# Closing stretch of a fused attention block: two more softmax-sum turns on TensorE, and a last chunk multiplied without token mixing

## The chip, the cores and the metric

The kernel runs on one core of one Trainium2 chip. The metric is the device time of that core in microseconds. Three runs of the kernel before gave 1424.36, 1424.47 and 1426.91 us, so the median is 1424.47 us.

## What is computed

The reference is a transformer block with adaptive layer normalisation, over 8 batches of 1024 tokens with 256 features, all in fp32. Cut to what matters here:

```python
h = _layernorm(x) * (1 + ca) + sa
x = x + ga * attention(h)              # 16 heads of 16, causal, w_out, b_out
h = _layernorm(x) * (1 + cb) + sb
x_prev = h shifted by one token (zero before the first)
xr = mu_r * h + (1.0 - mu_r) * x_prev
xk = mu_k * h + (1.0 - mu_k) * x_prev
r = sigmoid(xr @ W_r)
k_act = square(relu(xk @ W_k))
x = x + gb * (r * (k_act @ W_v))
```

`sa, ca, ga, sb, cb, gb` come from a small modulation matmul per batch. The softmax divides by the sum of the exponentials of a row; the kernel carries that sum as a seventeenth row beside the 16 rows of each head's output.

## The kernel before, in words

Tokens of a batch are cut into two chunks of 512 (`c` = 0, 1), heads into four groups of four (`g`); one group of one batch is a unit `u`, 32 in all. The unit's work is cut into steps. A maxima step (`maxima`) multiplies queries by keys into `pp` and lets VectorE (DVE) take the row maxima; a weights step (`weights`), nine steps later, multiplies again into `pw`, and ScalarE (ACT) makes exponentials `w` of it. `attend` multiplies `w` by the values into `po`; its sums go into a tile `o`. TensorE (PE) takes its instructions strictly in program order.

The program is a list of slots. In each slot `step` issues one weights step and one maxima step of a later unit, then what fell due in `soon`, then the slot's filling from hand-written tables (`PREP`, `POST`, `END`: the number is a slot, the name a piece of work), then `attend` of the step before. DMAs wrapped in `later` are issued at the start of the next slot. The last two units are `y` = 30 and `z` = 31, groups 2 and 3 of the last batch; their steps are interleaved and cut by `GROUPS_APART`. Slot 289 is the last with a maxima step; slots 290 to 298 hold weights steps alone.

The division by the softmax sum is made in one of two ways. `gather` writes `o` to DRAM and reads it back in another layout into `oT`; `spread_sums`, `invert`, `write_over`, `read_over` carry the sums through DRAM, and `divide` multiplies `oT` on GpSimd (POOL). `gather_last` stays on the chip: TensorE transposes `o` into `psum`, VectorE inverts the sums (`inv`) and widens them (`wide`), TensorE turns them back (`pinv`), VectorE multiplies `o`, and four DMAs put its heads into `oT`. Before the change only chunk 1 of units `y` and `z` goes the second way.

`post` then is the second half of the block for one chunk: `project` (`py`), statistics, normalisation (`hb`), `turn` (transposes `ptb`, then `h2T`), `mix` (the difference of neighbouring tokens, `step`, on POOL), `mixed` (the two mixtures on DVE: receptance in `mix`, key written over `step`), `receptance` (`pr`), `key` (`pk`, then the square on POOL) and `value` (`pkv`). Chunk 0 of the last batch is placed by `END` at slot 261 + n, its keys and values after the last slot. Chunk 1 has its own function `tail`, run last of all and worked in halves of 256 tokens so that engines overlap: `py`, statistics, `pt_last`, `h2T_last`, mixing on DVE, `pr`, `pk_last`, `pkv_last`, output.

PSUM has four one-bank buffers (`ps_t`) that `pw`, `po`, `py`, `pr`, `pk`, `pkv`, `psum` and `pinv` take in rotation, and two double ones (`ps_s`) for `pp`. A matmul whose bank has not been read out yet waits, and all matmuls behind it wait with it.

Of the kernel before, what the change touches and what calls it, by code (L numbers as in the profile page):

```python
# [69 lines left out]
def adaln_block(  # L70
# [24 lines left out]
    def bank(name):  # L95
        return ps_t.tile([P, CW], F32, tag="t", name=name)
# [38 lines left out]
    def later(f, steps=1, urgent=False):  # L135

        if strict[0]:
            due.append((clock[0] + steps, not urgent, f))
        else:
            f()  # L140
# [542 lines left out]
    def gather_last(u, c):  # L683

        o = U[u]["o", c]
        b, g = divmod(u, NG)
        pt = bank(f"psum{u}")
        for t in range(NT):
            pe.transpose(pt[:, t * P : (t + 1) * P], o[:, t * P : (t + 1) * P], ident)
        inv = sb.tile([P, NT, HG], F32, tag="few", bufs=2, name=f"inv{u}")  # L690
        dve.reciprocal(inv, pt.rearrange("p (t j s) -> p t j s", t=NT, s=ST)[:, :, :, HD])
        wide = sb.tile([P, NT, HG, ST], F32, tag="over", bufs=2, name=f"wide{u}")
        dve.tensor_copy(wide, inv.unsqueeze(3).to_broadcast([P, NT, HG, ST]))
        po = bank(f"pinv{u}")
        for t in range(NT):
            pe.matmul(
                po[:, t * P : (t + 1) * P],
                wide[:, t].rearrange("p j s -> p (j s)"),
                ident,
                start=True,  # L700
                stop=True,
            )
        dve.tensor_mul(o, o, po)
        for j in range(HG):
            at = (g % 2) * HG * HD + j * HD
            queue = act if j % 2 and u == B * NG - 1 else sync
            queue.dma_start(
                A[b, c]["oT"][at : at + HD, g // 2, :], o[j * ST : j * ST + HD, :]
            )

    def spread_sums(b, c, d):

# [24 lines left out]
    def divide(b, c, d):  # L737
        S = A[b, c]
        pool.tensor_mul(S["oT"][:, d, :], S["oT"][:, d, :], S["over", d])


    def post(b, c):
# [90 lines left out]
        def tail():  # L833

            def both(f):
                f(0)
                f(1)

            def columns(half):
                return slice(half * CW // 2, (half + 1) * CW // 2)

            both(lambda half: project(2 * half))
            st = sb.tile([P, NT, 6], F32, tag="st", bufs=2, name="st_last")
            mv = sb.tile([P, NT, 2], F32, tag="mv", bufs=2, name="mv_last")
            rs = sb.tile([P, NT], F32, tag="rs", bufs=2, name="rs_last")
            h = sb.tile([P, NT, D], F32, tag="h", bufs=2, name="h_last")

            def normal(half):  # L850
                ts = (2 * half, 2 * half + 1)
                for t in ts:
                    dve.bn_stats(st[:, t, :], S["x"][:, t, :])
                    dve.bn_aggr(mv[:, t, :], st[:, t, :])
                of = slice(2 * half, 2 * half + 2)
                dve.tensor_scalar_add(rs[:, of], mv[:, of, 1], EPS)
                pool.tensor_tensor(rs[:, of], rs[:, of], m_half[:, of], ALU.pow)
                for t in ts:
                    dve.tensor_scalar(
                        h[:, t, :],  # L860
                        S["x"][:, t, :],
                        mv[:, t, 0:1],
                        rs[:, t : t + 1],
                        ALU.subtract,
                        ALU.mult,
                    )

            both(normal)
            h2T = sb.tile([P, DC, CW + 1], F32, tag="h2T", name="h2T_last")
            pool.tensor_copy(h2T[:, :, 0:1], A[b, 0]["edge"])  # L870

            def turned(half):
                pt = bank(f"pt_last{half}")
                for d in range(DC):
                    for n in range(2):
                        pe.transpose(
                            pt[:, (d * 2 + n) * P : (d * 2 + n + 1) * P],
                            h[:, 2 * half + n, d * P : (d + 1) * P],
                            ident,
                        )  # L880
                for d in range(DC):
                    act.activation(
                        h2T[:, d, 1 + half * CW // 2 : 1 + (half + 1) * CW // 2],
                        pt[:, d * CW // 2 : (d + 1) * CW // 2],
                        AF.Identity,
                        bias=modT[:, SHIFT_B, d, b : b + 1],
                        scale=modT[:, SCALE_B, d, b : b + 1],
                    )

            both(turned)  # L890
            step = sb.tile([P, DC, CW], F32, tag="step", name="step_last")
            S["mix"] = sb.tile([P, DC, CW], F32, tag="mix", bufs=2, name="mix_last")

            def mixed_half(half):
                of = columns(half)
                for d in range(DC):
                    dve.tensor_sub(
                        step[:, d, of],
                        h2T[:, d, 1 + half * CW // 2 : 1 + (half + 1) * CW // 2],
                        h2T[:, d, of],  # L900
                    )
                for n in range(2):
                    for d in range(DC):
                        dve.scalar_tensor_tensor(
                            (S["mix"], step)[n][:, d, of],
                            step[:, d, of],
                            mus[:, n, d : d + 1],
                            h2T[:, d, of],
                            ALU.mult,
                            ALU.add,  # L910
                        )

            both(mixed_half)
            S["ka"] = sb.tile([P, DC, CW], F32, tag="mix", bufs=2, name="ka_last")

            def keys(half):
                of = columns(half)
                pk = bank(f"pk_last{half}").rearrange("p (e n) -> p e n", e=DC)
                for e in range(DC):
                    for d in range(DC):  # L920
                        pe.matmul(
                            pk[:, e, :],
                            wk_sb[:, d, e * P : (e + 1) * P],
                            step[:, d, of],
                            start=(d == 0),
                            stop=(d == DC - 1),
                        )
                ka = S["ka"][:, :, of]
                act.activation(ka, pk, AF.Relu)
                dve.tensor_mul(ka, ka, ka)  # L930

            both(lambda half: (receptance(2 * half), keys(half)))

            def values(half):
                t0 = 2 * half
                pv = bank(f"pkv_last{half}")
                rows(pv, S["ka"], G[b]["wv"], (t0, t0 + 1))
                r = S["r", t0]
                dve.scalar_tensor_tensor(r, r, 1.0, pv, ALU.add, ALU.mult)
                dve.tensor_add(flat(t0), flat(t0), r)  # L940
                (sync, act)[half].dma_start(
                    tokens(out, b, c)[:, t0 : t0 + 2, :], S["x"][:, t0 : t0 + 2, :]
                )

            both(values)

        return dict(
            load=load_xb,
# [60 lines left out]
    def finish(T, now):  # L1009
        u, k = T  # L1010
        attend(u, k)
        c, _, ends = groups_of(u)[k]
        if ends:
            b, g = divmod(u, NG)
            if u >= B * NG - 2 and c:
                soon.append((now + 1, lambda: gather_last(u, c)))
                return
            soon.append((now + 1, lambda: gather(u, c)))
            if g % 2:
                for n, f in enumerate((spread_sums, invert, write_over, read_over)):  # L1020
                    soon.append((now + 2 + n, lambda f=f: f(b, c, g // 2)))
                soon.append((now + 7, lambda: divide(b, c, g // 2)))
# [48 lines left out]
    22 m.k1; 22 n.q1; 24 n.k1; 26 n.v0; 28 n.v2  # L1071
    """
    END = """
    26 x.load; 28 x.bias; 32 x.project0; 32 x.project2; 33 x.stats0; 33 x.stats1; 34 x.norm0;
    34 x.norm1; 35 x.turn; 35 x.mix; 36 x.mixed00; 36 x.mixed01; 36 x.mixed10; 36 x.mixed11;
    36 y.load; 37 y.bias; 37 x.receptance0; 37 x.receptance2
    """

    def place(table, at, **of):
# [32 lines left out]
    for b in range(B):  # L1112
# [10 lines left out]
            fold0=lambda b=b: fold(b, 0),  # L1123
            fold1=lambda b=b: fold(b, 1),
        )
    place(END, at, x=ready[b][0], y=ready[b][1])


    mask = const.tile([P, CW], F32, tag="mask", name="mask")
# [60 lines left out]
        while soon and soon[0][0] <= clock[0]:  # L1190
            soon.pop(0)[1]()
    strict[0] = False
    for f in ("key0", "key1", "value0", "value2"):
        ready[B - 1][0][f]()
    ready[B - 1][1]["tail"]()

# [51 lines left out]
```

## Time and profile before

| what | value |
|---|---|
| median of three runs | 1424.47 us |
| the profiled execution's own time | 1423.17 us |
| its span, first to last instruction | 1421.4 us |
| PE busy in the span | 1392.2 us (98%) |
| DVE, ACT, POOL busy | 1059.2, 896.5, 548.7 us |
| mean granted TensorE clock | 0.992 |

The profile was taken in one execution. "Busy" counts the time in which an engine had an instruction in work; matmuls are pipelined, so a matmul's row is longer than the time from its start to the next start. An fp32 matmul leaves two records. PEclk is the share of full TensorE clock that was granted in a stretch. Line numbers in the trace are all L112, the line of the helper that records every instruction; so the rows are told apart by tile names. The rows of the timeline give start, duration, engine, operation, output and inputs, number of instructions, and in brackets the engine's idle time before them and what released it.

### The profile page before, as it was taken

The numbers are of one execution on the slowest core, as the hardware profiler recorded it, in microseconds if no ns is written. First come the engines' busy times: TensorE is split into PE (matmuls) and PEld (weight loads), VectorE is DVE, ScalarE is ACT, GpSimd is POOL, SyncE is SP. The second block draws the span as 40 slices with busy tenths as digits, with TensorE's granted clock in tenths as the row PEclk, the third lists the DMA queues.
The fourth block names the chain that finished last, engine by engine and source line by source line (L and its number), as shares of the span: only waits on it lengthen the run. The fifth ranks groups of instructions, "written<-read, shape, count | busy, mean of one in ns | idle before, by whom it ended". The sixth has DMA issues, their size and how long they took to land.

```text
span 1421.4 us, 29731 instructions
## 1 busy us (share of the span) xinstructions
PE 1392.2 (98%) x11256; PEld 736.5 (52%) x11256; DVE 1059.2 (75%) x2869; ACT 896.5 (63%) x1693; POOL 548.7 (39%) x840
## 2 busy tenths in 40 slices
PE   8999999999999999999999999999999999999997
PEld 4544455555554555555554555545555555455455
DVE  6777687788777877787777887777787877787334
ACT  3466676666676666666666666666667665576541
POOL 1142242445423454434424354234543343345441
PEclk9999999999999999999999999999999999999998
DMA  6513323222222323222242222223232221301111
GB/s 191 177 36 89 123 76 113 62 101 80 94 69 75 107 83 99 73 91 73 76 128 62 95 83 89 75 76 107 69 102 63 76 93 61 99 32 36 47 34 33
DMA packets 81270, 118.95 MB, mean 84 GB/s; under 512 B 10208, under 2 KB 38752, under 8 KB 81128
## 3 DMA queue, kind: packets, MB, share of 16 engines
q1 hardware_dynamic: 80792, 116.74, 25.9%
q8 instruction: 88, 1.44, 0.4%
q14 instruction: 54, 0.44, 0.1%
q10 hardware_dynamic: 336, 0.33, 0.1%
HBM read 71.17 MB, written 45.09 MB: 82 GB/s over the span
## 4 chain that ended last, share of the span: by engine, by line
PE 93%; DVE 3%; POOL 1%; ACT 1%; issue 1%; DMA 0%; ACTq 0%; POOLq 0%; SPq 0%; DVEq 0%
PE pw L112 11%; PE po L112 8%; PE pq L112 8%; PE pp L112 7%; PE po_e L112 5%; PE po_c L112 5%; PE py L112 4%; PE pkv L112 4%; PE pr L112 4%; PE pv L112 4%; PE pk L112 4%; PE pw_a L112 3%; PE pw_c L112 3%; PE pw_d L112 3%; PE pw_e L112 2%; PE pmx L112 2%
## 5 line engine op out<-in xcount | busy, mean ns | idle before, releaser
L112 DVE TENSOR_REDUCE max<-pp 128x2 f32<-128x1024 f32 x256 | 302.3, 1219 | 127.3 <-PE pp L112 126.3
L112 ACT ACTIVATE w<-pw 128x512 f32<-128x512 f32 x512 | 265.1, 603 | 88.9 <-PE pp L112 71.0
L112 PE MATMUL pw<-q,k 32*128 32x512 f32 x1024 | 265.5, 616 | 0.4 <-ACT w_i L112 0.4
L112 PE MATMUL pp<-k,q 32*128 32x512 f32 x1024 | 255.7, 620 | 0.0
L112 PEld LDWEIGHTS pw<-q,k 32*128 32x128 f32 x1024 | 110.4, 183 | 104.7 <-issue 64.2
L112 DVE CUSTOM_DVE_ANT_0 pp_d<-pp_d,mask 128x128 f32<-128x128 f32 x240 | 102.4, 437 | 64.4 <-PE pp_d L112 58.2
L112 DVE DVE_READ_ACCUMULATOR2_ANT max<- 128x1 f32 x1024 | 144.8, 141 | 0.0
L112 PE MATMUL po<-w,v 128*32 128x512 f32 x1024 | 123.1, 598 | 0.0
L112 DVE CUSTOM_DVE_ANT_0 pp_b<-pp_b,mask 128x128 f32<-128x128 f32 x240 | 102.4, 437 | 16.8 <-PE pp_b L112 10.1
L112 PE MATMUL pq<-hT,wqk_sb 128*128 128x512 f32 x240 | 113.7, 606 | 1.0 <-ACT hT L112 1.0
L112 DVE CUSTOM_DVE_ANT_0 pp_c<-pp_c,mask 128x256 f32<-128x256 f32 x240 | 103.2, 440 | 8.3 <-PE pp_c L112 2.2
L112 DVE CUSTOM_DVE_ANT_0 pp_e<-pp_e,mask 128x512 f32<-128x512 f32 x128 | 87.9, 708 | 20.4 <-PE pp_e L112 18.1
L112 DVE CUSTOM_DVE_ANT_0 pp_a<-pp_a,mask 128x512 f32<-128x512 f32 x128 | 87.9, 707 | 16.9 <-PE pp_a L112 14.7
L112 POOL TENSOR_TENSOR xb<-xb,r 128x512 f32<-128x512 f32 x30 | 41.4, 1378 | 141.0 <-DVE r L112 115.9
L112 ACT ACTIVATE w_a<-pw_a 128x512 f32<-128x512 f32 x128 | 66.2, 603 | 41.6 <-PE pp_a L112 40.3
L112 POOL TENSOR_TENSOR o<-o,more 128x512 f32<-128x512 f32 x62 | 79.1, 1276 | 26.1 <-ACT more L112 26.1
L112 POOL TENSOR_TENSOR rsb<-rsb,m_half 128x2 f32<-128x2 f32 x30 | 21.4, 714 | 169.0 <-DVE rsb L112 168.9
L112 PEld LDWEIGHTS pp<-k,q 32*128 32x128 f32 x1024 | 82.7, 183 | 6.1 <-DVE max L112 5.6
L112 ACT ACTIVATE w_e<-pw_e 128x512 f32<-128x512 f32 x128 | 66.3, 604 | 14.1 <-PE pp_e L112 13.3
L112 ACT ACTIVATE w_c<-pw_c 128x512 f32<-128x512 f32 x120 | 64.8, 596 | 16.3 <-PE pp_c L112 14.5
L112 ACT ACTIVATE w_d<-pw_d 128x512 f32<-128x512 f32 x120 | 62.3, 602 | 16.6 <-PE pp_d L112 12.9
L112 ACT ACTIVATE w_b<-pw_b 128x512 f32<-128x512 f32 x120 | 62.0, 603 | 16.8 <-PE pp_b L112 16.3
(207 smaller groups left out, 3031.9 us busy)
## 6 DMA issues: line engine op xcount, KB each, us to landing
od<-o SPq DMA_DIRECT2D x62, 256.0 KB
pad<-qk SPq DMA_DIRECT2D x60, 256.0 KB
q<-pad SPq DMA_DIRECT2D x30, 512.0 KB
k<-pad SPq DMA_DIRECT2D x30, 512.0 KB
xa<-in_x SPq DMA_DIRECT2D x16, 512.0 KB
xb<-in_x SPq DMA_DIRECT2D x16, 512.0 KB
oT<-od SPq DMA_DIRECT2D x62, 128.0 KB
ov<-over SPq DMA_DIRECT2D x31, 256.0 KB
```

Of the source, the lines that this page charges most:

```text
L112: made = f(*args, **kwargs)
```

## The change

`gather_last` now serves chunk 0 of units `y` and `z` too; for chunk 0 its four DMAs are issued one slot later. So the sums of that pair no longer go through DRAM, and `divide` falls away for it. The `END` table is moved forward: chunk 0 projects in slots 288 and 289 instead of 293, and its keys come in slots 297 and 298 instead of after the last slot; the load and the bias of its `x` come six slots earlier as well.

In `tail` the mixing is dropped. `folded`, in slot 294, makes four weight tiles on DVE: W_r and W_k times mu, and times one minus mu. Key and receptance are then sums of two products each, one with the tokens and one with the tokens before. The order on TensorE becomes: six filler matmuls (`warm`), transposes and keys of half 0, transposes and keys of half 1, then receptance and values of each half.

```diff
@@ gather_last
-        for j in range(HG):
-            at = (g % 2) * HG * HD + j * HD
-            queue = act if j % 2 and u == B * NG - 1 else sync
-            queue.dma_start(
-                A[b, c]["oT"][at : at + HD, g // 2, :], o[j * ST : j * ST + HD, :]
-            )
+        def side_by_side():
+            for j in range(HG):
+                at = (g % 2) * HG * HD + j * HD
+                queue = act if j % 2 and c and u == B * NG - 1 else sync
+                queue.dma_start(
+                    A[b, c]["oT"][at : at + HD, g // 2, :], o[j * ST : j * ST + HD, :]
+                )
+        if c:
+            side_by_side()
+        else:
+            later(side_by_side)
@@ new, before post
+    by_mu = []
+    def folded():
+        rest = sb.tile([P, 2, DC], F32, tag="rest", name="rest")
+        dve.tensor_scalar(rest, mus, -1.0, 1.0, ALU.mult, ALU.add)
+        for n, of in enumerate((wr_sb, wk_sb)):
+            both = sb.tile([P, DC, CW], F32, tag="hT", bufs=2, name=f"by_mu{n}")
+            pair = []
+            for m, factor in enumerate((mus, rest)):
+                w = both[:, :, m * D : (m + 1) * D]
+                for d in range(DC):
+                    dve.tensor_scalar_mul(w[:, d, :], of[:, d, :], factor[:, n, d : d + 1])
+                pair.append(w)
+            by_mu.append(pair)
@@ tail
-            both(turned)
-            step = ...; S["mix"] = ...
-            def mixed_half(half): ...          # 2 differences, 4 mixtures on DVE
-            both(mixed_half)
+            def here_and_before(half, d):
+                at = half * CW // 2
+                return h2T[:, d, 1 + at : 1 + at + CW // 2], h2T[:, d, at : at + CW // 2]
             def keys(half):
...
-                        pe.matmul(
-                            pk[:, e, :],
-                            wk_sb[:, d, e * P : (e + 1) * P],
-                            step[:, d, of],
-                            start=(d == 0),
-                            stop=(d == DC - 1),
-                        )
+                        for m, tokens_of in enumerate(here_and_before(half, d)):
+                            pe.matmul(
+                                pk[:, e, :],
+                                by_mu[1][m][:, d, e * P : (e + 1) * P],
+                                tokens_of,
+                                start=(d == 0 and m == 0),
+                                stop=(d == DC - 1 and m == 1),
+                            )
-            both(lambda half: (receptance(2 * half), keys(half)))
+            def receptances(half):             # 2 x DC x 2 matmuls of 128x256, then tanh
...
+            warm(6, "warm1")
+            turned(0)
+            keys(0)
+            turned(1)
+            keys(1)
-            both(values)
+            both(lambda half: (receptances(half), values(half)))
@@ finish
-            if u >= B * NG - 2 and c:
+            if u >= B * NG - 2:
                 soon.append((now + 1, lambda: gather_last(u, c)))
                 return
@@ END
-    26 x.load; 28 x.bias; 32 x.project0; 32 x.project2; 33 x.stats0; 33 x.stats1; 34 x.norm0;
-    34 x.norm1; 35 x.turn; 35 x.mix; 36 x.mixed00; 36 x.mixed01; 36 x.mixed10; 36 x.mixed11;
-    36 y.load; 37 y.bias; 37 x.receptance0; 37 x.receptance2
+    20 x.load; 22 x.bias; 27 x.project0; 28 x.project2; 29 x.stats0; 29 x.stats1; 30 x.norm0;
+    30 x.norm1; 30 y.load; 31 x.turn; 31 x.mix; 32 x.mixed00; 32 x.mixed01; 32 y.bias; 33 x.mixed10;
+    33 x.mixed11; 33 w.folded; 34 x.receptance0; 35 x.receptance2; 36 x.key0; 37 x.key1
@@ after the slots
-    for f in ("key0", "key1", "value0", "value2"):
+    for f in ("value0", "value2"):
```

In the `END` table `x` is chunk 0 and `y` chunk 1 of the last batch; these letters are not the units y and z.

More of the change, by code (lines that the diff above doesn't have):

```diff
@@ L888, in turned @@
                     )
-            both(turned)
[L891 to L897, printed above, removed]
-                        step[:, d, of],
-                        h2T[:, d, 1 + half * CW // 2 : 1 + (half + 1) * CW // 2],
-                        h2T[:, d, of],
-                    )
[L902 to L911, printed above, removed]
-            both(mixed_half)
+            def here_and_before(half, d):
+                at = half * CW // 2
+                return h2T[:, d, 1 + at : 1 + at + CW // 2], h2T[:, d, at : at + CW // 2]
             S["ka"] = sb.tile([P, DC, CW], F32, tag="mix", bufs=2, name="ka_last")
             def keys(half):
-                of = columns(half)
                 pk = bank(f"pk_last{half}").rearrange("p (e n) -> p e n", e=DC)
@@ L920, in keys @@
                     for d in range(DC):
-                        pe.matmul(
-                            pk[:, e, :],
-                            wk_sb[:, d, e * P : (e + 1) * P],
-                            step[:, d, of],
-                            start=(d == 0),
-                            stop=(d == DC - 1),
-                        )
-                ka = S["ka"][:, :, of]
+                        for m, tokens_of in enumerate(here_and_before(half, d)):
[6 more added lines that the diff above has]
+                            )
+                ka = S["ka"][:, :, columns(half)]
                 act.activation(ka, pk, AF.Relu)
                 dve.tensor_mul(ka, ka, ka)
-            both(lambda half: (receptance(2 * half), keys(half)))
+            def receptances(half):
+                pr = bank(f"pr_last{half}")
+                for n in range(2):
+                    for d in range(DC):
+                        for m, tokens_of in enumerate(here_and_before(half, d)):
+                            pe.matmul(
+                                pr[:, n * D : (n + 1) * D],
+                                tokens_of[:, n * P : (n + 1) * P],
+                                by_mu[0][m][:, d, :],
+                                start=(d == 0 and m == 0),
+                                stop=(d == DC - 1 and m == 1),
+                            )
+                r = sb.tile([P, CW], F32, tag="r", bufs=2, name=f"r_last{half}")
+                act.activation(r, pr, AF.Tanh, scale=0.5)
+                S["r", 2 * half] = r
+            warm(6, "warm1")
[3 more added lines that the diff above has]
+            keys(1)
             def values(half):
@@ L1125, in adaln_block @@
         )
-    place(END, at, x=ready[b][0], y=ready[b][1])
+    place(END, at, x=ready[b][0], y=ready[b][1], w=dict(folded=lambda: folded()))
     mask = const.tile([P, CW], F32, tag="mask", name="mask")
```

## The prediction

> **What bounds the kernel now.** I read the page's busy shares first, then the timeline of PE and DVE over the last 120 us, then the clock in stretches of 2 us, then the chain that ended last.
>
> ```profile
> PE 1392.2 (98%) x11256; PEld 736.5 (52%) x11256; DVE 1059.2 (75%) x2869; ACT 896.5 (63%) x1693; POOL 548.7 (39%) x840
> ```
>
> PE is the bound: work moved from one place of its queue to another saves nothing, work added costs its length, and only PE's idle time and slow clock can be won. Two stretches of the timeline show where VectorE runs behind PE:
>
> ```profile
> 1300.37 0.60 PE L112 MATMUL pmx<-ident,max 128*4 128x128 f32 x4
> 1301.96 0.70 DVE L112 CUSTOM_DVE_ANT_0 pp_e<-pp_e,mask 128x512 f32<-128x512 f32 x1
> 1302.58 0.14 DVE L112 DVE_READ_ACCUMULATOR2_ANT max<- 128x1 f32 x1
> ...
> 1314.17 2.36 DVE L112 TENSOR_REDUCE max<-pp 128x2 f32<-128x1024 f32 x2 [0.75 <-PE pp L112]
> 1314.30 0.59 PE L112 MATMUL pp<-k,q 32*128 32x512 f32 x2
> ```
>
> Slot 283's maxima products leave PE at 1300.44 (where the chain of waits lets pmx begin) and DVE at 1302.72; slot 286's leave PE at 1314.89 and DVE at 1316.5. What `gather_last` costs is seen where unit z runs it today:
>
> ```profile
> 1383.61 0.66 PE L112 MATMUL psum<-ident,o 128*128 128x128 f32 x4 [0.87 <-DVE o L112]
> 1384.31 0.26 DVE L112 RECIPROCAL inv<-psum 128x16 f32<-128x16 f32 x1 [0.75 <-PE psum L112]
> 1384.60 0.43 DVE L112 COPY wide<-inv 128x512 f32<-128x512 f32 x1
> 1385.17 1.13 PE L112 MATMUL pinv<-ident,wide 128*128 128x128 f32 x8 [0.90 <-DVE wide L112]
> ```
>
> PE stands 0.90 us between psum and pinv although DVE was free. The clock in 2 us stretches (columns: PE, PEld, DVE, ACT, POOL busy, then PEclk):
>
> ```profile
> 1340.00:1342.00 2.00, 2.00 (x3) 0.79 (x3) 0.00 (x0) 0.84 (x2) 0.66 (x1) 0.54 0.00 0
> 1366.00:1368.00 2.00, 2.00 (x6) 1.64 (x5) 0.00 (x0) 0.82 (x2) 0.75 (x2) 0.50 0.00 0
> 1404.00:1406.00 2.00, 2.00 (x6) 1.55 (x6) 2.00 (x6) 0.81 (x2) 0.00 (x0) 0.50 0.00 0
> ```
>
> Three times near the end PE works at half clock. The end of the chain:
>
> ```profile
> 1403.75 3.67 PE pr L112 x8
> 1407.42 2.28 PE pk_last L112 x8
> 1409.70 1.73 PE pr L112 x8
> 1411.43 1.73 PE pk_last L112 x8
> 1413.16 3.47 PE pkv_last L112 x16
> ```
>
> Eight records (four 128x256 matmuls) take 1.73 us at full clock, so 0.433 us a matmul; the first pr and pk pay 2.5 us for half clock.
>
> **The change, marker by marker.** I follow PE's queue and note its shift, after minus before.
>
> *First new turn, slot 283.* The changed order puts psum and pinv behind the slot's pp_e, and `inv` behind pp_e's reductions on DVE. Four transposes take 0.53 (as the four pmx), PE is done at 1300.97; `inv` starts when DVE is free, 1302.72; plus 0.29 to wide, 0.43, 0.14 to PE: pinv starts at 1303.58. PE stands 2.6 us. Pinv to the next matmul is 0.97: 1304.55. Shift **+4.1**. DVE's multiply of o waits for pinv, with mix and the next maxima queued behind it, so nothing is won back: pmx, pk, the buffer `step` that POOL may write only after pk, mix on DVE and the wait of pp_i for it (0.93 today) all move along. POOL gets the bias of x there (2.79, today in slot 289) ahead of w_g's masks; they end at about 1315.3 against PE's need at 1316.3: hidden with 1 us to spare, and costing what exceeds that. SP's four extra DMAs (0.58 each) stand behind the urgent mrow and before the `ov` read of the other chunk, which is needed microseconds later: nothing (2.3 if they stood in the way). The load of x, moved past the `over` write on SP, is issued near 1292, 20 us before its bias: nothing.
>
> *Second, slot 286.* PE is done with psum at 1319.0 + 0.53, DVE with the reductions at 1316.5 + 4.1 = 1320.6; plus 0.86 is 1321.46 and plus 0.97 is 1322.43, against 1314.89: **+7.5**, 1.9 us of it standing.
>
> *Slots 288, 289.* Both halves of py come here, 1.73 each; the oT DMAs (issued until about 1325.6) land before PE's 1330.9. The first py gives DVE time: pw_e and pp_3 took 2.80 instead of a usual 1.93, I take 0.87 back. **+10.1** at po_3.
>
> *Slots 290 to 293.* Normalisation now stands on ACT between w_i and the next exponentials, and pk (slot 292) needs the bank that the first of those frees. On POOL the square of ka (done 1337.40, so 1347.5) is followed by the two pow chains; today they take 1360.13 to 1362.71, so 1350.1. Two hb (0.98) end at 1351.2, the first exponential at 1351.8. Pk starts at 1351.85 instead of 1339.88: 1.84 us of new standing, **+12.0**. At full clock pk takes 1.73 instead of 3.42 (-1.7); ptb moves in (+1.0): **+11.3** at po_i. POOL's `step` (2.03) now stands before `o`, psum waits 0.7 longer: **+12.0**. Without py (-3.46), **+8.5** at pw in slot 294. DVE's eight weight products (3.0 us, at h_last's 0.74 for two) and the mixtures lie under slots 293 to 295, where DVE is mostly idle, and are ready some 25 us before the tail: nothing, 3.0 without that cover.
>
> *Slots 295, 296.* Today 1359.72 to 1370.90 (11.2): two pw steps bound by ACT with hb among them, 1.30 standing, pkv at half clock (3.78), ptb. With pr between the steps, ACT keeps up: 1.85 + 1.73 + 1.85 + 1.93 + 1.73 = 9.1. **+6.4**. *Slots 297, 298:* two pk (3.46) for two pr (3.65) and a wait of 0.54: **+5.8** when po_i ends (1382.74).
>
> *To the tail.* The turn to pinv's end takes 3.58 as today, then pk (3.46) and the waits for POOL's ka (1.2) are gone. But py now catches up with its DMAs: o was done at 1387.03 and the last packets moved in 1389.50 to 1389.75, 7.0 after po_i; pkv ends at 7.04. I allow 0.3 standing; py ends 10.9 after po_i instead of 15.6: **+1.1**.
>
> *The tail.* Today py's end (1398.35) to pkv_last's end (1416.45) is 18.1. After: first transposes 1.64 after py as today (the six warm matmuls, 1.3, fit in), ACT 0.9 later, 0.5 for the first half of h2T: keys start at 3.05. Then PE: keys 3.46, transposes 0.45, h2T 0.65, keys 3.46, receptance 3.46, values 1.73, receptance 3.46, values 1.73: 21.45. The mixing and the half clock are gone, but eight keys and eight receptance matmuls (6.9 us) are new: **+4.4**. The last add and the DMA are the same.
>
> So +4.4 with no half clock after 1300, against three such stretches today.
>
> **A rule against the trace.** The clock row first: at 1340 it fell to 0.54 though PE had stood only 0.44 us in the stretch before (ahead of pw, 1337.2 to 1337.6); what ran before were pw steps of 32 rows without pp. The Trainium skill, "TensorE: Matmul & The Clock Gate", section "HAM oscillation", says to avoid PE-idle gaps above about 3.4 us. By that rule the new stands of 2.6, 1.9 and 1.84 us cost no clock: +4.4. By the row, the low stretch of pw_i and pw_0 followed by 1.84 us of standing drops the clock as today, and pk gets its 1.7 back: **+6.1**. I follow the trace. A gap of 2.6 or 1.9 us among joint steps has no row (the 0.93 at 1305.7 left the clock at 1.00): each costs between 0 and 1.7, one half-clock stretch of 3.4 us like 1340 to 1343.3; a gain is excluded, since standing cannot raise a full clock. I take 0 for these, as the nearest row (0.93) says, and keep 3.4 for the range. Standing of 1.7 before the keys, with transposes in it, lies between 1.24 (0.28 and 0.96 before 1349.5, clock 1.00) and the 5.3 from 1398.35 to 1403.67, transposes inside, that dropped it today; I take full clock there, too, with 3.4 as the bad end.
>
> The profiled execution took 1423.17 with a span of 1421.4; the median is 1.3 above it. On the median: 1424.5 + 6.1 = **1430.6**.
>
> **Rivals.** *The stands are not there (not slower).* If DVE reaches `inv` and ACT reaches the exponentials before PE asks, 2.6 + 1.9 + 1.84 = 6.3 fall out of +4.4: 1422.6, and with the oT wait and h2T overlap gone as well (1.0) 1421.6. For it: PE is the only bound in the shares, and DVE had 1.19 and 0.75 idle there. Against: in both slots DVE ends 1.6 to 2.3 behind PE, and its order is fixed. It decides if DVE is less than 0.6 behind at psum. Chance 0.27; half-way versions make it "same", the full one "faster".
>
> *The clock pays more (slower still).* The new stands each bring a half-clock stretch, or the keys run at half clock as pr does today: +4.4 + 1.7 + 3.4 = +9.5, 1434.0. For it: three stretches today for smaller causes. Against: `warm` and full-array products are strewn where only pw was. Chance 0.23.
>
> *Main case,* +4 to +8: 0.50. That the change does not do what it says can be ruled out for the order: the DRAM route of these sums is gone from SP's queue.
>
> **Numbers.** 0.2% (2.85 us) is about what a measurement of this kernel can tell from no change. The likeliest is 1430.6. Of the first rival 0.11 lies below 1421.6 and 0.16 within 0.2%; of the main case 0.03 falls within 0.2%, the rest, 0.47, and the second rival's 0.23 are slower: faster 0.11, same 0.19, slower 0.70. The range runs from 1422.5 to 1436.5: about 0.13 is left out below, where both kinds of standing vanish, and 0.06 above, where more than the second rival's half-clock stretches come together.
>
> **What would show it.** Right: pinv in slots 283 and 286 stands 2 us or more behind DVE's wide; pk behind ACT in slot 292; py in the last turn behind a DMA; eight records of keys twice as many as before, at full clock, and 21 to 22 us from py to the last values. Wrong: pinv standing under 1 us, no standing at pk, a tail under 19 us, or an end of po_i shifted by less than 3 us.

## The result, and the profile after

The changed kernel took 1435.58 us (median of eight runs, 1430.96 to 1438.62) against 1426.10 us (1423.75 to 1431.04) for the kernel before on the same chip: ratio 1.0062, 95% interval 1.0048 to 1.0076. It is slower. Its profiled execution took 1430.96 us with a span of 1429.1 us; that is the shortest of the eight, so the profile shows the mildest case. Against the profiled execution before it is 7.8 us longer, against the medians 9.5.

From the page of the changed kernel, the shares (engine, busy us, share of the span, instructions):

```profile
PE 1397.6 (98%) x11324; PEld 742.4 (52%) x11324; DVE 1056.8 (74%) x2871; ACT 897.0 (63%) x1693; POOL 549.0 (38%) x839
```

PE has 68 records and 5.4 us of busy time more: 8 transposes, which leave one record each (`psum` x4 for four), and 30 matmuls with two. The span grew by 7.7. DVE is less busy than before, and is what PE waits for. PE's waits after 1290 us in the trace of after (engine, tile, releaser: us in total, times, longest):

```profile
PE pinv L112 <- DVE wide L112: 6.2, 4, 2.4
PE pk L112 <- ACT w L112: 1.7, 1, 1.7
PE pk_last L112 <- ACT h2T_last L112: 1.4, 2, 0.7
```

Before, `pinv` waited 1.9 in two times; two of the four are new. The first is in slot 283, here in the timelines of PE and of DVE of after:

```profile
1300.41 0.66 PE L112 MATMUL psum<-ident,o 128*128 128x128 f32 x4
1302.00 0.70 DVE L112 CUSTOM_DVE_ANT_0 pp_e<-pp_e,mask 128x512 f32<-128x512 f32 x1
1302.61 0.25 DVE L112 RECIPROCAL inv<-psum 128x16 f32<-128x16 f32 x1
1302.90 0.43 DVE L112 COPY wide<-inv 128x512 f32<-128x512 f32 x1
1303.47 1.13 PE L112 MATMUL pinv<-ident,wide 128*128 128x128 f32 x8 [2.41 <-DVE wide L112]
```

PE is through with `psum` at once; DVE must first finish the masked maxima, and the reciprocal starts at 1302.61. The second new turn, in slot 286, stands in the same way:

```profile
1322.92 1.13 PE L112 MATMUL pinv<-ident,wide 128*128 128x128 f32 x8 [1.80 <-DVE wide L112]
```

The third row of the waits is in the tail; the second is this (timeline of ACT, then PE, after):

```profile
1351.12 1.09 ACT L112 ACTIVATE hb<-xb,awayb,rsb 128x256 f32<-128x256 f32 x2 [0.17 <-POOL awayb L112]
1352.11 2.03 ACT L112 ACTIVATE w<-pw 128x512 f32<-128x512 f32 x4
1352.74 3.66 PE L112 MATMUL pk<-step,wk_sb 128*128 128x512 f32 x4 [1.71 <-ACT w L112]
```

ACT normalises `hb` before the exponentials that free the bank of `pk`. The clock in stretches of 2 us (PE, PEld, DVE, ACT, POOL busy, PEclk, DMA):

```profile
1312.00:1314.00 2.00, 2.00 (x13) 1.59 (x10) 1.90 (x8) 0.79 (x2) 2.00 (x3) 0.50 0.03 8
1354.00:1356.00 2.00, 2.00 (x3) 0.65 (x3) 0.00 (x0) 0.15 (x1) 0.00 (x0) 0.50 0.00 0
1406.00:1408.00 2.00, 2.00 (x11) 1.76 (x10) 0.58 (x2) 0.00 (x0) 0.00 (x0) 1.00 0.03 8
```

The first of these stretches in the kernel before:

```profile
1312.00:1314.00 2.00, 2.00 (x34) 1.20 (x28) 1.42 (x4) 0.58 (x1) 1.16 (x1) 1.00 0.00 0
```

Half clock near 1312 is new; near 1354 it stands at the same `pk` as at 1340 before; in the tail, at half clock from 1401 to 1408 before, the clock is now full. The tail in PE's timeline of after:

```profile
1398.36 3.83 PE L112 MATMUL py<-wob,oT 128*128 128x256 f32 x16
1402.02 1.50 PE L112 MATMUL warm<-ident 128*128 128x128 f32 x12
1403.78 0.78 PE L112 MATMUL pt_last<-ident,h_last 128*128 128x128 f32 x4 [0.26 <-DVE h_last L112]
1405.22 3.72 PE L112 MATMUL pk_last<-h2T_last,by_mu 128*128 128x256 f32 x16 [0.66 <-ACT h2T_last L112]
1408.78 0.60 PE L112 MATMUL pt_last<-ident,h_last 128*128 128x128 f32 x4
1410.09 3.72 PE L112 MATMUL pk_last<-h2T_last,by_mu 128*128 128x256 f32 x16 [0.71 <-ACT h2T_last L112]
```

And the end of the chain of waits of after, for the five lines shown of before:

```profile
1410.09 3.72 PE pk_last L112 x16
1413.81 3.45 PE pr_last L112 x16
1417.26 1.73 PE pkv_last L112 x8
1418.99 3.45 PE pr_last L112 x16
1422.44 1.74 PE pkv_last L112 x8
```

Each set of keys or receptances has 16 records for 8 before, at full clock: 3.45 us where a set took 1.73. `py` ends at 1402.2, the last values at 1424.18: 22.0 us for 18.1 before.

### The profile page after: what moved, and what is told of

Its sections match the earlier page's. It is cut to its first block, busy times and chain, and to the rows that moved or that the text cites. A ratio compares the mean times of both kernels' runs of the same rounds, so it can differ in the third digit from the quotient of the medians.

```text
span 1429.1 us, 29864 instructions
## 1 busy us (share of the span) xinstructions
PE 1397.6 (98%) x11324; PEld 742.4 (52%) x11324; DVE 1056.8 (74%) x2871; ACT 897.0 (63%) x1693; POOL 549.0 (38%) x839
## 4 chain that ended last, share of the span: by engine, by line
PE 93%; DVE 3%; POOL 1%; ACT 1%; DMA 1%; issue 1%; SPq 0%; DVEq 0%; POOLq 0%; ACTq 0%
PE pw L112 11%; PE po L112 8%; PE pq L112 8%; PE pp L112 7%; PE po_e L112 5%; PE po_c L112 5%; PE py L112 4%; PE pkv L112 4%; PE pk L112 4%; PE pv L112 4%; PE pr L112 4%; PE pw_a L112 3%; PE pw_c L112 3%; PE pw_d L112 3%; PE pw_e L112 3%; PE pmx L112 2%
## 5 line engine op out<-in xcount | busy, mean ns | idle before, releaser
L112 DVE CUSTOM_DVE_ANT_0 pp_b<-pp_b,mask 128x128 f32<-128x128 f32 x240 | 102.3, 437 | 17.0 <-PE pp_b L112 10.2
L112 POOL TENSOR_TENSOR rsb<-rsb,m_half 128x2 f32<-128x2 f32 x30 | 21.5, 715 | 168.7 <-DVE rsb L112 168.7
```

The costliest lines, as they stand in the source:

```text
L112: made = f(*args, **kwargs)
```

## Experiments

The theory was that three places, each by itself, make the loss: the two stands at the reciprocals, `pk` behind ACT, and the tail's doubled matmuls. The rivals were that the clock is the cause, or that the parts cost only together. Every kernel was timed in five rounds beside the kernel before on its chip; the medians of the kernel before were 1427.49 us for the first four kernels, 1426.58 for the next four, 1426.41 for the last three.

### The turns alone, and the tail alone

```diff
@@ e1: kernel before, only finish() and gather_last as changed; END and tail of before
-            if u >= B * NG - 2 and c:
+            if u >= B * NG - 2:
```

> Only the two new turns of the softmax sums; END table and tail as before the change. My theory (each new turn holds PE for its own 1.5 us of work and for 1.8 to 2.4 us behind VectorE's maxima): +7.5 us at slot 287 and to the end, because nothing later is taken off PE: ratio to before 1.0053, span near 1429, with pinv waiting 2.4 and 1.8 us on wide. Rival (PE idle is absorbed later, since PE waits for VectorE or ScalarE anyway in slots 285 to 298): only the work of 2 x 1.5 us remains, +3.0 us, ratio 1.0021, and waits of pp_i, pw or pkv elsewhere shrink by as much as pinv waits.

Measured 1435.45 us, ratio 1.0057 (1.0043 to 1.0071). The two new waits are there as in after: 2.41 and 1.80 us. So the turns alone lose nearly as much as the whole change, where nothing is drawn forward in `END`.

```diff
@@ e2: kernel before, only folded() and the new tail
+    33 w.folded
-            both(turned) ... mixed_half ... receptance, keys
+            warm(6, "warm1"); turned(0); keys(0); turned(1); keys(1); receptances, values
```

> Only the new tail (weights times mu made in slot 294, filler matmuls, no mixing); sums and END as before the change otherwise. My theory (6.9 us of added matmuls outweigh the mixing and the half clock of the old tail): py's end to the last values 21.5 us instead of 18.1, +3.4 us, ratio 1.0024. Rival (the mixing on VectorE was the longer path of the tail, and the loss of the change comes from the turns and the schedule alone): the tail gets shorter by 2 us or so, ratio 0.9985.

Measured 1432.54 us, ratio 1.0033 (1.0021 to 1.0046): the tail loses by itself. Its profiled execution ran at a mean clock of 0.846, its other runs at 0.989 to 0.994, so I read nothing from its profile. The two losses sum to 1.0090, more than the 1.0062 of the whole. The forward `END` table, which only the whole has, wins some of it back: in the trace of after PE is 11.15 us late in slot 289 and 3.85 us late when the last `py` ends.

### Is it the clock?

```diff
@@ e3: after without the fillers of the tail
-            warm(6, "warm1")
```

> The changed kernel without the six filler matmuls in the tail. My theory (PE standing from the end of py to the first keys, about 3 us with two transposes in it, lets the clock fall as in the tail of before): granted clock 0.5 in the keys, the tail 1.7 to 3.4 us longer than 22.1 us of the profile of after, ratio to before about 1.008 to 1.009. Rival [...]the clock stays full, ratio as for the change, 1.006.

Measured 1434.62 us, ratio 1.0049 (1.0032 to 1.0065), not distinguishable from after's 1.0062. My theory fell. PE's timeline of this kernel:

```profile
1400.11 3.80 PE L112 MATMUL py<-wob,oT 128*128 128x256 f32 x16
1405.52 0.78 PE L112 MATMUL pt_last<-ident,h_last 128*128 128x128 f32 x4 [1.60 <-DVE h_last L112]
1406.95 3.72 PE L112 MATMUL pk_last<-h2T_last,by_mu 128*128 128x256 f32 x16 [0.66 <-ACT h2T_last L112]
1424.01 1.89 PE L112 MATMUL pkv_last<-wvb,ka_last 128*128 128x256 f32 x8
```

The keys take the same 3.72 us after 1.60 us of standing as after the fillers. The fillers bought nothing that shows. The slow stretch of the old tail is in all four profiles that were read with that tail (before, e1, e7, e11) and in none of the eight whose keys start about 3 us after `py`, with fillers or without. So the earlier start, and not PE being kept busy in between, is the likely end of it.

```diff
@@ e4: after, with fillers in front of the three new waits
         po = bank(f"pinv{u}")
+        if not c:
+            for n in range(10 if g == 2 else 8):
+                pe.matmul(po[:, :P], ident, ident, start=True, stop=True)
@@ and eight more such matmuls, into a buffer of pp, ahead of slot 292's pk
```

> The changed kernel with filler matmuls of 128x128 put on PE where it stands: ten and eight between psum and pinv of the two new turns, eight ahead of pk in slot 292. They lie inside the stands (2.2, 1.7 and 1.7 us of work), so by themselves they cost 0 to 0.3 us. If the stands make the clock fall (my theory from the row at 1340 us): no half-clock stretch after 1300, pk in slot 292 takes 1.9 instead of 3.66 us, pkv in slot 285 1.99 instead of 2.82, span 2 to 3 us below the 1429.1 of after at equal other stretches, ratio to before about 1.004. Rival (the fall comes from pw steps alone or from elsewhere, standing has no part): half-clock stretches remain, ratio 1.006 to 1.0065.

Measured 1431.63 us, ratio 1.0031 (1.0018 to 1.0044). That is half of the loss, and would be the share of the clock. The profile does not bear this out. Waits of PE after 1290, and two stretches of the clock, both of this kernel:

```profile
PE pinv L112 <- DVE wide L112: 2.0, 2, 1.1
```

```profile
1310.00:1312.00 2.00, 2.00 (x20) 1.76 (x16) 1.97 (x7) 0.00 (x0) 2.00 (x3) 0.50 0.16 46
1352.00:1354.00 2.00, 2.00 (x11) 2.00 (x11) 0.00 (x0) 2.00 (x5) 0.30 (x1) 0.50 0.00 0
```

The new stands are filled, and in this execution the clock falls at both places all the same. So a stand is not needed for a fall. The other executions say something else, though: the mean granted clock of e4's ten lies at 0.993 to 0.999, that of after's eight at 0.988 to 0.996. The lower times go with a higher clock; whether the fillers raised it is not shown.

### Each stand taken away

```diff
@@ e5: pinv of chunk 0 in a function of its own, one slot after psum
-        (pinv directly after wide)
+                if c == 0:
+                    soon.append((now + 2, lambda: turned_back(u, c)))
@@ END (and the last receptance of the chunk before goes from slot 289 to 288)
-    27 x.project0; 28 x.project2;
+    28 x.project0; 28 x.project2;
```

> The changed kernel with pinv and what follows it one slot later than psum in the two new turns, so that VectorE has a slot's time for inv and wide; for the DMAs' sake receptance of the chunk before is moved from slot 289 to 288 and both py to 289. My theory (2.4 and 1.8 us of standing behind VectorE are the cost that the turns need not have): both waits of pinv on wide fall under 0.3 us, -4.2 us against the change, ratio to before 1.0032. Rival (VectorE is the bound of these slots): the standing shows up again at pp, pw or pkv, gain under 1.5 us, ratio 1.005 or more.

Measured 1429.19 us, ratio 1.0018 (1.0011 to 1.0026): 4.4 thousandths, some 6 us, below after, for 4.2 us of waits taken away (6.2 to 2.0); the rest is taken up under "The clock in these comparisons". Waits of PE in this kernel:

```profile
PE pinv L112 <- DVE wide L112: 2.0, 2, 1.1
PE pk L112 <- ACT w L112: 1.7, 1, 1.7
```

The wait of `pp_i` for the maxima, 0.9 in before and after, is 0.2 here: DVE got its delay hidden, and PE's next demand finds it further on.

```diff
@@ e6: after, hb of the last batch's chunk 0 on VectorE
-            if strict[0]:                       # norm on ACT
+            if strict[0] and tag != f"b{B - 1}_0":
```

> The changed kernel with chunk 0's last normalisation on VectorE instead of ScalarE (slot 291). My theory (hb waits for POOL's pow chain and holds the exponentials, so that pk in slot 292 waits for a bank): the wait of 1.71 us at pk is gone, and with it part of the half clock there: -1.7 to -3.4 us against the change, ratio 1.0037 to 1.005. Rival (POOL's chain, not ScalarE's order, holds that place): pk or ptb waits as long for something else, ratio 1.006.

Measured 1429.80 us, ratio 1.0030 (1.0020 to 1.0040), 3.2 thousandths below after. The wait at `pk` is gone from the list, and that `pk` takes 1.98 us for 3.66, at full clock. But this profile has another half-clock stretch that after has not, over the second new turn (PE's timeline, then the clock):

```profile
1353.45 1.98 PE L112 MATMUL pk<-step,wk_sb 128*128 128x512 f32 x4
```

```profile
1324.00:1326.00 2.00, 2.00 (x12) 1.77 (x15) 0.22 (x1) 0.00 (x0) 0.00 (x0) 0.52 0.00 0
```

So moving one instruction group to the engine that is idle there takes away 1.7 us of stand. The 1.7 us of clock gained at `pk` came back elsewhere, and the span is only 1.0 us shorter (1428.1 for 1429.1).

```diff
@@ e7: after, with the tail of before and without folded()
```

> The changed kernel with the tail of before (mixing on VectorE, no filler, plain weights, none folded); the turns and the forward END stay. My theory (the folded tail costs 3.4 to 4 us more than the mixed one even with the mixed one at half clock): tail 18.1 us from py's end to the last values, 3.4 to 4 us less than the change, ratio 1.0035 to 1.004. Rival (the new tail pays): ratio 1.008.

Measured 1431.06 us, ratio 1.0033 (1.0020 to 1.0046). PE's timeline:

```profile
1403.42 3.80 PE L112 MATMUL py<-wob,oT 128*128 128x256 f32 x16
1411.44 0.97 PE L112 MATMUL pt_last<-ident,h_last 128*128 128x128 f32 x4 [1.85 <-DVE h_last L112]
1412.49 3.35 PE L112 MATMUL pr<-wr_sb,mix_last 128*128 128x256 f32 x8
1420.87 3.62 PE L112 MATMUL pkv_last<-wvb,ka_last 128*128 128x256 f32 x16
```

The old tail starts its matmuls on mixed tokens 5.3 us after `py` ends (1407.2), pays half clock in the first set (3.35 for 1.89), and is still done at 1424.5: 17.3 us, 4.7 less than the folded one.

### The three mended

If the places are independent, mending all of them should beat the kernel before. In the tail only the first keys gain from folded weights, since they need not wait for DVE's mixing; by the time the rest is due, the mixtures can be ready:

```diff
@@ e8, e9: e5 and e6 together, and in the tail (abridged)
-            turned(0); keys(0); turned(1); keys(1); then receptances and values by halves
+            turned(0); differences(0); keys_by_mu(half 0); turned(1)   # folded weights
+            mixed_half(0, receptance); differences(1); mixed_half(1, key)
+            squared(0); mixed_half(1, receptance)                      # mixed by DVE
+            receptance(0); keys_mixed(half 1); squared(1)
+            values(0); receptance(2); values(1)
```

> All together: pinv one slot later, the normalisation on VectorE, and a tail that uses folded weights only for the keys of the first half (they start before any mixing is done) and mixes the rest, with the six fillers. By my sums: -4.2 - 1.7 against the change, and the tail 15.7 us instead of 22.1 (keys 3.46, one receptance 1.73, mixed keys 1.73, values 1.73, receptance 1.73, values 1.73, transposes and starts): about -12 us, 3 us below before: ratio 0.997 to 0.998. Rival (gains overlap, VectorE becomes the bound of the tail): tail 18 us or more, ratio 1.000 or above.

Measured 1418.38 us, ratio 0.9943 (0.9922 to 0.9964). This kernel does not compute the block: the second half's receptance is mixed from a buffer that the key mixture has overwritten. The next one writes the key mixture elsewhere (into the first half's columns of `step`, free by then) and is otherwise the same:

> The changed kernel with three mends: the first chunks' turned sums come back one slot later, the last first chunk's norm is on VectorE, and the tail computes only the first half's keys by the folded weights (half of a chunk, 256 tokens) and mixes for all else. Unlike the run before it, the second half's receptance is mixed from its own differences. Theory A (the three savings add, each at its own place): ratio 0.994, as there, 8 us below the kernel before; tail from the last projection's end 15.8 us. Rival B (the gain of that run hung on the order of VectorE's writes in the tail): the tail is 1 us or more longer and the ratio 0.995 or above.

Measured 1418.54 us, ratio 0.9955 (0.9937 to 0.9973): faster than the kernel before, and so than the changed one. The ratio is just inside the rival's figure, but the rival's mechanism is not there, as PE's timeline of this kernel shows:

```profile
1306.53 1.16 PE L112 MATMUL pinv<-ident,wide 128*128 128x128 f32 x8
...
1392.28 3.78 PE L112 MATMUL py<-wob,oT 128*128 128x256 f32 x16
1395.89 1.50 PE L112 MATMUL warm<-ident 128*128 128x128 f32 x12
1397.65 0.78 PE L112 MATMUL pt_last<-ident,h_last 128*128 128x128 f32 x4 [0.26 <-DVE h_last L112]
1399.09 2.00 PE L112 MATMUL pk_last<-h2T_last,by_mu 128*128 128x256 f32 x8 [0.66 <-ACT h2T_last L112]
1400.92 0.60 PE L112 MATMUL pt_last<-ident,h_last 128*128 128x128 f32 x4
1401.36 1.89 PE L112 MATMUL pk_last<-h2T_last,by_mu 128*128 128x256 f32 x8
1403.09 1.89 PE L112 MATMUL pr<-wr_sb,mix_last 128*128 128x256 f32 x8
1404.82 1.89 PE L112 MATMUL pk_last<-step_last,wk_sb 128*128 128x256 f32 x8
...
1409.99 1.89 PE L112 MATMUL pkv_last<-wvb,ka_last 128*128 128x256 f32 x8
```

`pinv` has no bracket, so nothing was waited for; the tail runs from 1396.1 (1392.28 + 3.78) to 1411.9 (the last values, 1409.99 + 1.89), 15.8 us, without a gap after the first keys. It is the old mixing done under four folded matmuls of extra work instead of sixteen.

Which part brings the gain? Two more kernels part it:

```diff
@@ e10: kernel before with e9's tail (and w.folded at slot 33), no turns, END of before
@@ e11: after with e5's and e6's edits, and the tail of before
```

> The kernel before with its last units' chunks gathered as they were, no new turns, and only the tail of the mended kernel (first half's keys by folded weights, the rest mixed; two folds more at slot 33). Theory A (the mended tail is worth its 18.1 minus 15.8 us and the rest of the mended gain comes from the turns): ratio 0.998 to 0.999. Rival B (the tail is the whole of the mended gain and the turns are worth nothing even when mended): 0.9945 to 0.996.

> The changed kernel with the turned sums one slot later and the last first chunk's norm on VectorE, and the tail as it was before (all mixed, no folded weights). Theory A (the turns cost time only by the two stands at the end of the reciprocals and the late norm; with those gone the earlier projections gain): ratio 0.9950 to 0.9965. Rival B (turns alone, even without stands, only add their matmuls): 1.000 to 1.002.

e10 measured 1424.74 us, ratio 0.9991 (0.9979 to 1.0004): the mended tail alone cannot be told from no change. e11 measured 1420.20 us, ratio 0.9960 (0.9947 to 0.9973). So the gain comes with the turns and the forward `END`, once PE does not stand for the reciprocals and `hb` is out of ACT's way. They bring the projection of chunk 0 some slots forward, and the `pkv` waits of before (1.3 behind ACT's `w_e`, 1.2 behind POOL's `ka`) are absent from e9's and e11's lists.

### The clock in these comparisons

Each execution has its own mean granted clock, and within one kernel the time follows it: the eight runs of after go from 1430.96 us at 0.996 to 1438.62 at 0.988. Fitted over all runs on record but e2's profiled one, with one slope for all and a level for each kernel, 0.001 of clock goes with 1.1 us. From that follows an estimate of what each kernel costs at the same clock, good to about 1 us, and only if lost clock costs the same in all of them:

| kernel | against | us at the same clock |
|---|---|---|
| after | before | about +10 |
| e1, turns only | before | +7.3 |
| e2, tail only | before | +6.4 |
| e3, no fillers in the tail | after | 0.0 |
| e4, stands filled | after | -0.7 |
| e5, `pinv` later | after | -3.8 |
| e6, norm on DVE | after | -1.5 |
| e7, old tail | after | -4.7 |
| e9, all mended | before | -2.5 |
| e10, mended tail only | before | +0.6 |
| e11, turns mended, old tail | before | -2.1 |

So e5 and e6 give back about the waits they take away (4.2 and 1.7), e7 gives back the 4.7 us that its tail is shorter, and what e4, e5 and e6 gain beyond this is a higher clock. Of the 7.9 us that e9 wins over the kernel before, about 2.5 are saved work and waiting; the rest is clock, on the mean 0.994 for 0.990. A kernel brings its clock with it, so the medians stand, but which edit keeps the clock up was not tried apart.

## Why the prediction was right

It forecast slower, 1430.6 us by the median then known, and the ratio of 1.0043 that this was (6.1 over 1424.47) came out as 1.0062. The way and the waits were right; the size was short by a third on the medians, outside the +4 to +8 of its main case. Point by point, as shifts on PE's queue in the profiled executions:

- *First turn.* 4.1 forecast, 4.07 measured (`pmx` at 1304.44 for 1300.37); the stand 2.6 forecast, 2.41 measured. The reading that DVE is behind at that place, though 75% busy over the span, was what counted.
- *Second turn.* 3.4 more forecast, 3.5 measured; stand 1.9 against 1.80.
- *The clock between them.* I took nothing for a fall behind the stands and kept 3.4 us for the range. The clock fell at 1312 and cost 1.55 us (`po_g` is 5.62 late, at 4.07 ahead of it). This is the term that was mis-sized. The reason that I gave for the bad end, the stand, is not shown to be the cause, though: the fall is there in e5, e9 and e11, where the stand is gone.
- *Slots 288 and 289.* The 0.87 that DVE wins back under the first `py` came (1.97 for 2.80), and a second 0.84 that I had not seen, in slot 287: `po_3` stood at +11.15 for +10.1.
- *`pk` in slot 292.* 1.84 forecast, 1.71 measured, and half clock with it as I took from the trace: 3.66 for the 3.49 of before. The clock there is not certain: in e6 and e9 the same `pk` ran at full clock.
- *Slots 293 to 298.* +8.8 at the end of `po_i`, where the working and the 1.7 of clock said 7.5. The difference is the 1.05 carried from `po_3`, 0.1 in the working's own sum (6.4 less 0.73 is 5.7, not 5.8), and small change.
- *`py` behind its DMAs.* I allowed 0.3; no wait shows, and the last packets moved at 1398.25 to 1398.50, at its start. `py` ended at +3.85 for 2.8.
- *The tail.* 21.45 forecast, 22.0 measured, keys starting 3.03 after `py` for 3.05. From the first keys' start to the second's are 4.87 for 4.56, since the transposes and the second wait for `h2T_last` take longer than the 1.1 I put; the other 0.2 is spread over the later sets and the pipeline's end. Full clock there was right.

The profile's sum is +7.7 for +6.1: 1.1 before the tail, 0.5 in it. That it came so near is in part luck, since the 1.55 of the unforeseen fall and the unforeseen 0.84 won back offset each other. The medians differ by 9.5; in the other seven runs of after the mean granted clock was 0.988 to 0.994 for the profiled run's 0.996, so I take the other 1.8 for more such half-clock stretches, which was argued and not shown stretch by stretch.

Of the rivals, *the stands are not there* is what e5 and e6 build: they take back some 6.3 and 4.6 us on the medians, 3.8 and 1.5 at the same clock. *The clock pays more* has the size (9.5 on the medians), but in the profile not the mechanism: the second new stand brings no fall, and the keys run at full clock. The first rival's number holds, too: it put 1421.6, 2.9 us below the median, with the folded tail in it; without that tail's 3.35 this is about 6.2 below, and e11, which has the old tail and no new stands, measured 6.2 us below the kernel before. Part of this agreement is luck. That working has no half clock at `pk` and in slots 295 and 296, and e11's profile, from one of its longer runs (1425.98 us at 0.990), still has it from 1348.9 to 1352.3 and from 1359.1 to 1369.3.

On the rule that I weighed: the Trainium skill, "TensorE: Matmul & The Clock Gate", section "HAM oscillation", warns of idle gaps above about 3.4 us. The 1.60 us of standing in e3's tail left the clock full, as the rule has it. The fall near 1312 needed no gap. In e9, the three microseconds before the fall and those of it (columns as above):

```profile
1308.00:1311.00 3.00, 2.79 (x17) 1.21 (x16) 2.93 (x10) 1.25 (x3) 3.00 (x5) 1.00 0.00 0
1311.00:1314.00 3.00, 3.00 (x15) 2.01 (x10) 2.83 (x14) 1.03 (x2) 2.75 (x4) 0.56 0.17 36
```

PE was idle 0.21 us. The measurement decides, as it did for `pk`.

## What to carry to other kernels

An engine that is 75% busy can be late exactly where a new step asks for it: before putting a round trip between PE and DVE into an in-order queue, read on the timeline when DVE gets to it there, and put the second half of the trip one step later. Weights folded to save a mixing on another engine double the matmuls; on a kernel that PE bounds this pays only for the matmuls that would otherwise wait for the mixing, here the first of four sets. Only the traces show that gain, 15.8 us of tail in e9 for 17.3 in e11; the times of these two cannot be told apart. A change that loses may hold a gain behind two stands: cost the stands apart from the idea before it is put aside.

## What was not expected of the hardware

The granted clock falls to half for 3.4 us, or for two or three times that (e7 and e11 have 10.2 us near 1360). Idle time of PE just before is no guide: in the 3.4 us before a fall it was 0.2 us in e9 at 1311, and 1.7 us in after at 1352.7.

In each of the twelve profiles read, all falls begin a whole number of 3.41 us apart. In after they begin at 21.5, 1311.8 and 1352.7 us, which are 378 and then 12 such steps. So the times at which a fall can begin look like a grid that runs through the execution, whatever the program does. Where the grid lies against PE's queue sorts the falls of slot 285. Counted from the start of `pp_i` there, a grid point lies between 0.04 us before and 2.43 us after it in the nine profiles that fall (after, e1, e3 to e7, e9 and e11), and at 2.49 in e8, 2.76 in before and 2.94 in e10, which do not. e8 has the new turns and no fall, so they do not decide alone, and that the kernel before was spared in its profile may be chance. The step from 2.43 to 2.49 is small, and nothing was run to move the grid, so this is a reading of the traces and not a test.

Leaving out the tail's fillers in e3 did not let the clock fall. Filling the stands in e4 did not keep it up at either place in the profiled execution, while the mean clock of its runs was higher than after's; what fillers do there stays open.
